# A perceiver layer on one core: first products regrouped, a slice of the shared expert by seven products, ranks computed earlier, two weight loads in chunks

## The chip, the cores and the metric

The kernel runs on one core of a Trainium2 chip. The time is the device time of that core in microseconds, as the median over several runs. One run was profiled: its time and the span of its trace are given beside each other below.

## The reference

The layer updates 256 tokens `x` of width 512 in three steps, all in float32. A layernorm without weights goes ahead of each step.

```python
x = x + xattn(layernorm(x), ctx, ctx)   # ctx: 25088 rows of width 512
x = x + attn(layernorm(x))              # 16 heads of 64, one key/value head, causal
x = x + ffn(layernorm(x))               # shared expert + top 8 of 64 experts

# xattn: qp = q@Wq.T+bq (128 wide), kp = k@Wk.T+bk, vp = v@Wv.T+bv
#        sigmoid(qp@kp.T / sqrt(128)) @ vp
# ffn:   shared = (silu(h@Sg) * (h@Su)) @ Sd * sigmoid(h@shared_gate)      inner width 1024
#        w, idx = top_k(softmax(h@gate_w), 8), w divided by its sum
#        expert e: (silu(h@Ge) * (h@Ue)) @ De, inner width 256, weighted by w
```

## The kernel before

**Cross attention** takes up most of the time. The context is cut into groups: group 0 has 128 rows (`HEAD`), groups 1 to 65 have 384 rows, three blocks of 128. For each group the keys are `pk = Wk @ context.T` (`keys`, eight matmul records of width 384 for a full group), evicted by ScalarE with the bias to `kT` (L362). The scores of a block are one product of a 128-column piece of `kT` with the queries `qT`; ScalarE applies the sigmoid and writes `zT` (L380). The value product `zT.T @ context` has 256 x 384 x 512 terms in blocks of 2 x 3 x 3 and is done with 15 block products instead of 18 (`PRODUCTS`, six PSUM banks named `xacc`): VectorE, GpSimd and ScalarE form sums of context blocks (`T`) and VectorE sums of score blocks (`S`). Group 0 has one block and only seven products (`FIRST_PRODUCTS`). The order of everything here is written out by hand: `in_turn` pins an instruction behind what was traced before it on its engine. In iteration `g` TensorE does the scores of the group's first two blocks, four products of the group before, the scores of the third block, the keys of group `g + 1`, then the other products of the group before. In iteration 1 the group before is group 0. VectorE turns group `g + 2`'s rows around in 32 x 32 squares (`quarters` to `cT`, L317) at the end of an iteration; the first two groups are turned by TensorE.

The loads of context go out on SP's queue, three groups ahead (`load_quarters`, four transfers, and `load_context`, one). The weights of later stages are fetched on the same queue during the cross attention: `later` makes a tile and a `fetch` that first lets GpSimd copy one element of the current `zT` into the tile's first element and then issues the transfers, so that they do not start early. `wvT` (1 MB) is fetched in group 6 and `a_wqT` (2 MB) in group 8. All of SP's transfers share that queue.

**Self attention** follows (from about 560 to 607 us), then routing and the **feed-forward stage**. Here most instructions are not pinned: the compiler's scheduler orders each engine's stream by when it expects operands. A shared expert of inner width 1024 is treated as four slices ("s", 0) to ("s", 3) of width 256, then eight experts ("e", 0) to ("e", 7) chosen by count are computed for all tokens ("whole" experts), with seven further experts (`FEW`) for a few gathered tokens. For each, `gate_up` makes 32 records of width 256 in two PSUM banks, ScalarE a sigmoid, VectorE two multiplications (L1217, L1218). `down` then multiplies with the down weights. For names in `SEVEN` the hidden values are first scaled per token (L1220), and the 2 x 2 block product is done in seven products of width 256 instead of eight: `sums_for_seven` forms four sums of weights on GpSimd (`t_s`, `t_e`) and four sums of hidden blocks on VectorE (`s_s`, `s_e`), the products accumulate in two double banks (`seven`), and `add_seven` adds them to `y` once, at the end. The scale of the shared slices is one row, written to memory by `turn_weights` and read back by a transfer on GpSimd's queue. Slice 0 is not in `SEVEN`: it goes down in four products of width 512 (`pd_s`, L1372), weighted by VectorE into `y` (L1381), and its gate products are made early (`ph_first`). `run` makes the next name's hidden values before the last one's down projection.

[...] In this stage four of them are handed out in turn by `bank`, so which instruction waits for which depends on the order of the calls.

`counted` ranks the 64 experts by their tokens, `permuted` gathers the weights in that order (`wso`). `seated`, called after expert 0's `gate_up`, counts each token's rank within each of the few experts (products `pn`, `rank`), compares it with the slot numbers (`share`, in the tile `fTf`), transposes that (`pt_share`) and gathers the tokens' rows by an indirect transfer. The weights of slices and experts rotate through three rooms (`wpool`), so slice 3's loads wait for slice 0's rooms, expert 0's for slice 1's, and so on.

Of the kernel before, what the change touches and what calls it, by code (L numbers as in the profile page):

```python
# [9 lines left out]
F32 = mybir.dt.float32  # L10
AF = mybir.ActivationFunctionType
ALU = mybir.AluOpType
# [9 lines left out]
def tile_perceiver_layer(  # L22
# [82 lines left out]
    def rows(src):  # L105
        return src.rearrange("(c p) f -> p c f", p=P)
# [7 lines left out]
    def blocks_of(g):  # L114

        return range(J) if g > 0 else (1,)
# [57 lines left out]
    def all_of(src):  # L174
        return (lambda t: t), src

    wvT_sb, fetch_wv = later("wvT", [P, ND, D], all_of(rows(wvT)))
    bv_sb, fetch_bv = later("bv", [P, D], all_of(bv[0].partition_broadcast(P)))
    a_wqT_sb, fetch_aq = later("a_wqT", [P, ND, INNER], all_of(rows(a_wqT)))
    a_wkv_sb, fetch_akv = later("a_wkv", [P, ND, 2 * DH], all_of(rows(a_wkvT)))  # L180
    a_wout_sb, fetch_aout = later("a_wout", [P, NE, D], all_of(rows(a_woutT)))
    ln_g_sb, fetch_lng = later("ln_g", [P, ND], all_of(ln_g))
# [162 lines left out]
    def keys(g):  # L345

        cT = turned_tiles.pop(g)
        n = len(blocks_of(g)) * P
        w = wkT_sb if g >= BY_PE else wk_plain_sb
        pk = keys_bank(f"pk_{g}")[:, 0:n]  # L350
        for c in range(ND):
            in_turn(
                nc.tensor.matmul(  # L353
                    pk,
                    lhsT=w[:, c, :],
                    rhs=cT[:, c, 0 : n // R, :].rearrange("p b r -> p (b r)"),
                    start=(c == 0),
                    stop=(c == ND - 1),
                )
            )  # L360
        kT = cpool.tile([QK, J * P], F32, tag="kT", name=f"kT_{g}")
        in_turn(nc.scalar.activation(kT[:, 0:n], pk, AF.Identity, bias=bk_sb))  # L362
        return kT

    def scores(g, kT, zT, blocks):
# [262 lines left out]
    for g in range(G):  # L628
        if g + 3 < G:
            load_quarters(g + 3)  # L630
            load_context(g + 3)
        named.z = zT = cpool.tile([P, J, T], F32, tag="zT", name=f"zT_{g}", bufs=3)
        context_sums(g, named)
        blocks = blocks_of(g)
        scores(g, kT, zT, blocks[0:2])
        if before is not None:
            values(before, 0, 4)
        if len(blocks) > 2:
            scores(g, kT, zT, blocks[2:3])
        if g + 1 < G:  # L640
            kT = keys(g + 1)
        if before is not None:
            values(before, 4)
        query_sums(g, named)
        if BY_PE <= g + 2 < G:
            turn(g + 2)
        for fetch in in_group.get(g, ()):
            fetch(zT[0:1, 0, 0:1])
        before, named = named, Named(g + 1)
        if g + 1 < G:  # L650
            context_sums_aside(g + 1, named)
# [140 lines left out]

    SEVEN = [("s", k) for k in range(1, NS)] + [("e", k) for k in range(WHOLE - 1)]
    LAST = ("e", WHOLE - 1)
    weights = {}
    scales = {}
# [377 lines left out]
    def turn_weights():  # L1177
        pt = bank("pt_wt")
        for t in range(NT):
            nc.tensor.transpose(pt[0 : E + 1, t * P : (t + 1) * P], wt[:, t, :], ident)  # L1180
        nc.vector.tensor_copy(wT, pt[0 : E + 1, :T])
        nc.gpsimd.dma_start(weights_of_tokens, wT)
        nc.gpsimd.dma_start(*spread(scale_rooms[0], slice(E, E + 1)))
        for k in range(1, NS):
            scales["s", k] = scale_rooms[0]

    def gate_up_products(n, halves, lo, hi, mark=lambda ins: ins):
        gu, _ = weights[n]
        for half, ph in enumerate(halves):
            if half > 0 and n == SEVEN[0]:  # L1190
                turn_weights()
            for f in range(NI):
                col = half * I + f * P
                for c in range(ND):
                    mark(
                        nc.tensor.matmul(  # L1196
                            ph[:, f * T + lo : f * T + hi],
                            lhsT=gu[:, c, col : col + P],
                            rhs=fT[:, c, lo:hi],
                            start=(c == 0),  # L1200
                            stop=(c == ND - 1),
                        )
                    )

    def gate_up(n, tiles_done=None):

        nm = f"{n[0]}{n[1]}"
        if tiles_done is None:
            halves = [bank(f"ph_{nm}_{half}") for half in range(2)]
            gate_up_products(n, halves, 0, T)  # L1210
        else:
            halves = tiles_done
        pg, pu = halves
        hT = hidden.tile([P, NI, T], F32, tag="hT", name=f"hT_{nm}")
        hf = hT.rearrange("p f t -> p (f t)")
        nc.scalar.activation(hf, pg, AF.Sigmoid)
        nc.vector.tensor_mul(hf, pg, hf)  # L1217
        nc.vector.tensor_mul(hf, pu, hf)  # L1218
        if n in SEVEN:
            nc.vector.tensor_mul(hT, hT, scales.pop(n).unsqueeze(1).to_broadcast([P, NI, T]))  # L1220
            sums_of[n] = sums_for_seven(n, hT)
        elif n == LAST:
            nc.vector.tensor_mul(hT, hT, scales.pop(n).unsqueeze(1).to_broadcast([P, NI, T]))
        return hT

# [33 lines left out]
        y11 y11 + u3  # L1261
    """
    HALF = D // 2
    sums_of = {}
    spread_out = {}
    seven = []

    def block(n, hT, dn, s, t, nm):
        i, k = nm[1:2], nm[2:3]
# [80 lines left out]
    def down(n, hT, parts=WIDE_PARTS):  # L1350
        if n in SEVEN:
            down_by_seven(n, hT)
            return
        _, dn = weights.pop(n)
        if n == LAST:
            for t, lo, hi in parts:
                pd = spread_out.pop((t, lo))
                for f in range(NI):
                    nc.tensor.matmul(  # L1359
                        pd,  # L1360
                        lhsT=hT[:, f, t * P : (t + 1) * P],
                        rhs=dn[:, f, lo:hi],
                        start=False,
                        stop=(f == NI - 1),
                    )
                nc.vector.tensor_add(y[:, t, lo:hi], pd, y[:, t, lo:hi])
            return
        nm = f"{n[0]}{n[1]}"
        for t, lo, hi in parts:
            pd = bank(f"pd_{nm}_{t}_{lo}")[:, 0 : hi - lo]  # L1370
            for f in range(NI):
                nc.tensor.matmul(  # L1372
                    pd,
                    lhsT=hT[:, f, t * P : (t + 1) * P],
                    rhs=dn[:, f, lo:hi],
                    start=(f == 0),
                    stop=(f == NI - 1),
                )
            w = wsh[:, t, :] if n[0] == "s" else wso[:, t, n[1] : n[1] + 1]
            so_far = x2 if n == ("s", 0) else y  # L1380
            nc.vector.scalar_tensor_tensor(  # L1381
                y[:, t, lo:hi], pd, w, so_far[:, t, lo:hi], ALU.mult, ALU.add
            )

    def run(names, between, last=WIDE_PARTS):

        pending = None
        for i, n in enumerate(names):
            hT = gate_up(n, first if n == ("s", 0) else None)
            if pending is not None:  # L1390
                down(*pending)
            pending = (n, hT)
            if i in between:
                between[i]()
        down(*pending, last)


    order = late.tile([1, E], mybir.dt.int32, tag="order", name="order")
# [105 lines left out]
            yield k, first, n * QUARTER  # L1504
            first += n * QUARTER

    def seated():


        w = wso[:, :, WHOLE : WHOLE + FEW]  # L1510
        chose = few.tile([P, NT, FEW], F32, tag="chose", name="chose")
        nc.vector.tensor_scalar(chose, w, 0.0, None, ALU.is_gt)
        ahead = few.tile([P, P], F32, tag="ahead", name="ahead")
# [4 lines left out]
        for t in range(NT):  # L1518
            for s in range(t + 1):
# [4 lines left out]
                    start=(s == 0),  # L1524
                    stop=(s == t),
                )

        rank = few.tile([P, NT, FEW], F32, tag="rank", name="rank")
        nc.vector.scalar_tensor_tensor(  # L1529
            rank.rearrange("p t i -> p (t i)"),  # L1530
            pn[:, 0 : NT * FEW],
# [3 lines left out]
            ALU.mult,  # L1535
        )
        nc.vector.tensor_scalar(rank, rank, 1.0, None, ALU.subtract)
        for t in range(NT):
            for r in range(NR):
                for k, first, n in slots_of_round(r):  # L1540
                    i = k - WHOLE
                    nc.vector.tensor_scalar(
                        share[:, t, r, first : first + n],
                        slot_sb[:, 0:n],
                        rank[:, t, i : i + 1],
                        w[:, t, i : i + 1],
                        ALU.is_equal,
                        ALU.mult,
                    )
# [128 lines left out]

    def few_added(r):
        for t, i, room in parts_of_round(r):  # L1680
            in_turn(
                nc.vector.scalar_tensor_tensor(
                    y[:, t, :], room, fetched_w[:, t, i : i + 1], y[:, t, :], ALU.mult, ALU.add
                )
            )

# [36 lines left out]
    def remaining(lo):  # L1723
# [5 lines left out]
        with tc.If(n_left > lo):  # L1729
            places(lo, hi, by=ACT)  # L1730
            store(nc.scalar, WIDE_PARTS)
            remaining(hi)

    places(
        0,
        WHOLE,
# [90 lines left out]
```

## Time and profile before

| | us |
|---|---|
| median of 3 runs (769.94 to 770.69) | 770.08 |
| the profiled execution: its time | 770.29 |
| its span in the trace | 768.5 |
| TensorE busy | 758.1 |
| VectorE busy | 565.3 |
| ScalarE busy | 201.2 |
| GpSimd busy | 198.2 |

The mean granted TensorE clock is 0.997 of full speed. In the profile, PE is TensorE's matmuls and PEld its weight loads, DVE is VectorE, ACT ScalarE, POOL GpSimd, and SPq the queue of transfers that SP issues. A float32 product shows as two records. Line numbers such as L353 are those of the kernel before. The span divides into the cross attention (to about 550 us), the change to the value projection and self attention (to about 607), the output normalisation and routing (to about 625), the shared slices (625 to 660), the experts (660 to 757) and the last sums and stores.

### The profile page before, as it was taken

Reading aid. Unit: us, or ns where it says so; the run is one execution under the profiler, and the core shown is the slowest. Engines: PE = TensorE matmul, PEld = TensorE weight load, DVE = VectorE, ACT = ScalarE, POOL = GpSimd, SP = SyncE. Lnnn points to the kernel's source line nnn. Section 1 sums busy time; section 2 is a strip of 40 time slices with the busy share of each in tenths; the row PEclk is TensorE's granted clock in tenths of the full one; section 3 lists DMA queues with packets and bytes.
Section 4 is the critical chain, followed back from the end, with each engine's and each line's share of the span. In section 5 each row is a group of like instructions: output and inputs, shape, how many; then the busy total and the mean of one; then the engine's idle time right before and its main releaser. Section 6 shows DMA issues by size and latency. Waiting matters only on the chain.

```text
span 768.5 us, 12420 instructions
## 1 busy us (share of the span) xinstructions
PE 758.1 (99%) x4056; PEld 619.8 (81%) x4056; DVE 565.3 (74%) x1652; ACT 201.2 (26%) x485; POOL 198.2 (26%) x361
## 2 busy tenths in 40 slices
PE   8999999999999999999999999999999999999996
PEld 6888888888888888888888888888876588887665
DVE  5988888888888888888888888888666575442353
ACT  4222222222222222222222222222346430010110
POOL 3222322322322322322322322322124213151150
PEclk9999999999999999999999999999999999999998
DMA  9999999899778778878778778770060025569940
GB/s 249 269 236 252 255 205 295 241 228 222 187 181 209 186 185 208 185 182 209 185 185 208 184 185 204 187 185 22 21 226 1 15 77 174 178 217 397 385 145 31
DMA packets 155190, 145.92 MB, mean 190 GB/s; under 512 B 7926, under 2 KB 113667, under 8 KB 155120
## 3 DMA queue, kind: packets, MB, share of 16 engines
q1 hardware_dynamic: 153088, 140.41, 70.4%
q0 software_dynamic: 1360, 4.13, 1.8%
q8 instruction: 34, 0.56, 0.3%
q10 hardware_dynamic: 672, 0.52, 0.2%
q14 instruction: 36, 0.29, 0.1%
HBM read 143.40 MB, written 1.64 MB: 189 GB/s over the span
## 4 chain that ended last, share of the span: by engine, by line
PE 97%; DVE 1%; ACT 0%; POOL 0%; issue 0%; ACTq 0%
PE xacc L572 37%; PE pk L353 22%; PE pz L371 11%; PE ph_e L1196 7%; PE seven L1302 4%; PE ph_s L1196 3%; PE pw L937 2%; PE pa L871 2%; PE ph_few L1618 1%; PE ps L963 1%; PE ptp L1014 1%; PE pi L204 1%; PE po_few L1649 1%; PE py L731 1%; PE ph_first L1196 0%; PE pd_few L1359 0%
## 5 line engine op out<-in xcount | busy, mean ns | idle before, releaser
L572 PE MATMUL xacc<-T,S 128*128 128x172 f32 (+2 forms) x912 | 185.5, 308 | 0.0
L353 PE MATMUL pk<-cT,wkT_sb 128*128 128x384 f32 x512 | 175.5, 486 | 0.0
L572 PEld LDWEIGHTS xacc<-T,S 128*128 128x128 f32 x912 | 152.6, 190 | 20.3
L353 PEld LDWEIGHTS pk<-cT,wkT_sb 128*128 128x128 f32 x512 | 97.1, 190 | 54.4
L539 POOL TENSOR_TENSOR T<-ctx 128x172 f32<-128x172 f32 x65 | 31.9, 491 | 384.9 <-PE xacc L572 379.3
L317 DVE STREAM_TRANSPOSE cT<-quarters 128x1536 f32<-128x1536 f32 x64 | 113.4, 1772 | 0.3 <-issue 0.2
L539 DVE TENSOR_TENSOR T<-ctx 128x172 f32<-128x172 f32 (+1 forms) x262 | 113.3, 433 | 0.0
L539 DVE TENSOR_TENSOR S<-zT 128x128 f32<-128x128 f32 x196 | 56.4, 288 | 72.2 <-ACT zT L380 72.2
L371 PE MATMUL pz<-qT,kT 128*128 128x256 f32 x392 | 106.0, 379 | 0.7 <-ACT kT L362 0.7
L380 ACT ACTIVATE zT<-pz 128x256 f32<-128x256 f32 (+1 forms) x131 | 64.2, 490 | 114.1 <-PE pz L371 114.1
L572 PE MATMUL xacc<-T,zT 128*128 128x173 f32 (+1 forms) x396 | 89.9, 308 | 0.0
L572 PE MATMUL xacc<-ctx,S 128*128 128x172 f32 x392 | 78.5, 309 | 0.0
L362 ACT ACTIVATE kT<-pk,bk 128x384 f32<-128x384 f32 (+1 forms) x66 | 38.1, 578 | 146.9 <-PE pk L353 146.9
L539 DVE TENSOR_TENSOR S<-zT,S 128x128 f32<-128x128 f32 x325 | 76.4, 285 | 0.0
L549 ACT COPY T<-ctx 128x170 f32<-128x170 f32 (+1 forms) x130 | 43.2, 333 | 125.4 <-PE xacc L572 124.0
L539 POOL TENSOR_TENSOR T<-ctx,T 128x170 f32<-128x170 f32 (+1 forms) x130 | 72.5, 576 | 2.2 <-PE xacc L572 2.2
L371 PEld LDWEIGHTS pz<-qT,kT 128*128 128x128 f32 x392 | 68.6, 190 | 4.8 <-ACT kT L362 1.3
L539 DVE TENSOR_TENSOR T<-ctx,T 128x172 f32<-128x172 f32 x195 | 65.4, 361 | 8.2 <-PE xacc L572 1.5
L572 PEld LDWEIGHTS xacc<-T,zT 128*128 128x128 f32 x396 | 66.4, 190 | 0.1
L572 PEld LDWEIGHTS xacc<-ctx,S 128*128 128x128 f32 x392 | 62.8, 190 | 0.0
L572 PE MATMUL xacc<-ctx,zT 128*128 128x170 f32 (+1 forms) x264 | 59.5, 307 | 0.0
L1196 PE MATMUL ph_e<-fT,gu 128*128 128x256 f32 x256 | 58.0, 382 | 0.3 <-DVE rank L1529 0.3
(297 smaller groups left out, 778.0 us busy)
## 6 DMA issues: line engine op xcount, KB each, us to landing
ctx<-in_context SPq DMA_DIRECT2D x65, 768.0 KB, 5.4
quarters<-in_context SPq DMA_DIRECT2D x256, 192.0 KB, 6.4
gu<-in_e_gate_up SPq DMA_DIRECT2D x12, 1024.0 KB, 9.9
dn<-in_e_down SPq DMA_DIRECT2D x11, 512.0 KB, 9.4
gu_s<-in_s_gate_up SPq DMA_DIRECT2D x8, 512.0 KB, 4.6
a_wqT<-in_a_wqT SPq DMA_DIRECT2D x1, 2048.0 KB, 15.6
a_wout<-in_a_woutT SPq DMA_DIRECT2D x1, 2048.0 KB, 15.6
dn_s<-in_s_down SPq DMA_DIRECT2D x4, 512.0 KB, 7.5
```

The source lines that it names most:

```text
L317: in_turn(nc.vector.transpose(new_turned(g), q.rearrange("p b (c r) -> p c b r", r=R)))
L353: nc.tensor.matmul(pk, lhsT=w[:, c, :], rhs=cT[:, c, 0 : n // R, :].rearrange("p b r -> p (b r)"), start=(c == 0), stop=(c == ND - 1),)
L362: in_turn(nc.scalar.activation(kT[:, 0:n], pk, AF.Identity, bias=bk_sb))
L371: nc.tensor.matmul(pz[:, i * T : (i + 1) * T], lhsT=kT[:, at : at + P], rhs=qT, start=True, stop=True,)
L380: nc.scalar.activation(zT[:, blocks[0] : blocks[-1] + 1, :].rearrange("p j t -> p (j t)"), pz[:, 0 : len(blocks) * T], AF.Sigmoid, scale=1 ...
L539: in_turn(f(o_, a_, b_))
L549: in_turn(nc.scalar.copy(named[to][:, 0:n], named[x_][:, 0:n]))
L572: nc.tensor.matmul(banks_of_products[i][:, cols], lhsT=named[lhs], rhs=named[rhs][:, 0:n],  start=i not in opened, stop=(g == G - 1 and last),
L871: nc.tensor.matmul(pa[:, 0 : hi - lo], lhsT=a_wqT_sb[:, c, e * P : (e + 1) * P], rhs=anT[:, c, lo:hi], start=(c == 0), stop=(c == ND - 1),)
L937: nc.tensor.matmul(pw[t], lhsT=oT[:, e, t * P : (t + 1) * P], rhs=a_wout_sb[:, e, :], start=(e == 0), stop=(e == NE - 1),)
L1196: nc.tensor.matmul(ph[:, f * T + lo : f * T + hi], lhsT=gu[:, c, col : col + P], rhs=fT[:, c, lo:hi], start=(c == 0), stop=(c == ND - 1),)
L1302: nc.tensor.matmul(product_of_seven(nm), lhsT=block(n, hT, dn, s_, t_, lhs), rhs=block(n, hT, dn, s_, t_, rhs),  start=(n == SEVEN[0] and ...
```

## The change

Four places change.

1. Iteration 1 of the cross attention deals the seven products of group 0 differently: two ahead of group 1's first scores, three between its scores, two after the next keys. The evictions of the keys of groups 1 and 2 are done in two pieces, the first 128 columns and then the others.
2. `wvT` and `a_wqT` are loaded by four transfers each, one for each chunk of 128 input rows, instead of one each.
3. Slice ("s", 0) joins `SEVEN`. Its scaling and its sums are made in slice 1's `gate_up`, ahead of slice 1's own (`weigh`), and its down projection follows slice 2's `gate_up`, with slice 1's behind it. `y` is no longer written by slice 0; the first of the few experts' additions takes `x2` in its place.
4. The part of `seated` that computes `rank` becomes `ranked_tokens`, called ahead of the whole experts' stage.

```diff
+    def by_chunks(src):
+        return [
+            ((lambda t, c=c: t[:, c, :]), src[c * P : (c + 1) * P, :]) for c in range(ND)
+        ]
-    wvT_sb, fetch_wv = later("wvT", [P, ND, D], all_of(rows(wvT)))
+    wvT_sb, fetch_wv = later("wvT", [P, ND, D], *by_chunks(wvT))
-    a_wqT_sb, fetch_aq = later("a_wqT", [P, ND, INNER], all_of(rows(a_wqT)))
+    a_wqT_sb, fetch_aq = later("a_wqT", [P, ND, INNER], *by_chunks(a_wqT))
...
-        in_turn(nc.scalar.activation(kT[:, 0:n], pk, AF.Identity, bias=bk_sb))
+        for lo, hi in ((0, P), (P, n)) if 0 < g < 3 else ((0, n),):
+            in_turn(nc.scalar.activation(kT[:, lo:hi], pk[:, lo:hi], AF.Identity, bias=bk_sb))
...
+        early, middle = (2, 5) if g == 1 else (0, 4)
+        if before is not None:
+            values(before, 0, early)
         scores(g, kT, zT, blocks[0:2])
         if before is not None:
-            values(before, 0, 4)
+            values(before, early, middle)
...
-            values(before, 4)
+            values(before, middle)
...
-    SEVEN = [("s", k) for k in range(1, NS)] + [("e", k) for k in range(WHOLE - 1)]
+    SEVEN = [("s", k) for k in range(NS)] + [("e", k) for k in range(WHOLE - 1)]
...
-            if half > 0 and n == SEVEN[0]:
+            if half > 0 and n == ("s", 1):
                 turn_weights()
...
+        if n == ("s", 1):
+            weigh(*waiting)
+        if n in SEVEN + [LAST] and n != ("s", 0):
+            weigh(n, hT)
+        return hT
+
+    def weigh(n, hT):
+        nc.vector.tensor_mul(hT, hT, scales.pop(n).unsqueeze(1).to_broadcast([P, NI, T]))
         if n in SEVEN:
-            nc.vector.tensor_mul(hT, hT, scales.pop(n).unsqueeze(1).to_broadcast([P, NI, T]))
             sums_of[n] = sums_for_seven(n, hT)
...
-        pending = None
+        pending = []
         for i, n in enumerate(names):
             hT = gate_up(n, first if n == ("s", 0) else None)
-            if pending is not None:
-                down(*pending)
-            pending = (n, hT)
+            if n == ("s", 0):
+                waiting.extend((n, hT))
+            elif n != ("s", 1):
+                for each in pending:
+                    down(*each)
+                pending = []
+            pending.append((n, hT))
...
-    def seated():
+    rank = few.tile([P, NT, FEW], F32, tag="rank", name="rank")
+    w = wso[:, :, WHOLE : WHOLE + FEW]
+
+    def ranked_tokens():
...
+            so_far = x2 if (r, i) == (0, ROUNDS[0][0][0] - WHOLE) else y
...
+    ranked_tokens()
     places(
```

More of the change, by code (lines that the diff above doesn't have):

```diff
@@ L1183, in turn_weights @@
         nc.gpsimd.dma_start(*spread(scale_rooms[0], slice(E, E + 1)))
-        for k in range(1, NS):
+        for k in range(NS):
             scales["s", k] = scale_rooms[0]
@@ L1218, in gate_up @@
         nc.vector.tensor_mul(hf, pu, hf)
+        if n == ("s", 1):
[5 more added lines that the diff above has]
+        nc.vector.tensor_mul(hT, hT, scales.pop(n).unsqueeze(1).to_broadcast([P, NI, T]))
         if n in SEVEN:
-            nc.vector.tensor_mul(hT, hT, scales.pop(n).unsqueeze(1).to_broadcast([P, NI, T]))
             sums_of[n] = sums_for_seven(n, hT)
-        elif n == LAST:
-            nc.vector.tensor_mul(hT, hT, scales.pop(n).unsqueeze(1).to_broadcast([P, NI, T]))
-        return hT
     S_OF_SEVEN = """
@@ L1263, in tile_perceiver_layer @@
     HALF = D // 2
+    spread_out = {}
     sums_of = {}
-    spread_out = {}
-    seven = []
+    seven, waiting = [], []
     def block(n, hT, dn, s, t, nm):
@@ L1378, in down @@
                 )
-            w = wsh[:, t, :] if n[0] == "s" else wso[:, t, n[1] : n[1] + 1]
-            so_far = x2 if n == ("s", 0) else y
+            w = wso[:, t, n[1] : n[1] + 1]
             nc.vector.scalar_tensor_tensor(
-                y[:, t, lo:hi], pd, w, so_far[:, t, lo:hi], ALU.mult, ALU.add
+                y[:, t, lo:hi], pd, w, y[:, t, lo:hi], ALU.mult, ALU.add
             )
     def run(names, between, last=WIDE_PARTS):
-        pending = None
+        pending = []
         for i, n in enumerate(names):
             hT = gate_up(n, first if n == ("s", 0) else None)
-            if pending is not None:
-                down(*pending)
-            pending = (n, hT)
+            if n == ("s", 0):
[5 more added lines that the diff above has]
+            pending.append((n, hT))
             if i in between:
                 between[i]()
-        down(*pending, last)
+        for each in pending:
+            down(*each, last)
     order = late.tile([1, E], mybir.dt.int32, tag="order", name="order")
@@ L1505, in slots_of_round @@
             first += n * QUARTER
-    def seated():
-        w = wso[:, :, WHOLE : WHOLE + FEW]
+    rank = few.tile([P, NT, FEW], F32, tag="rank", name="rank")
+    w = wso[:, :, WHOLE : WHOLE + FEW]
+    def ranked_tokens():
         chose = few.tile([P, NT, FEW], F32, tag="chose", name="chose")
@@ L1526, in seated @@
                 )
-        rank = few.tile([P, NT, FEW], F32, tag="rank", name="rank")
         nc.vector.scalar_tensor_tensor(
@@ L1537, in seated @@
         nc.vector.tensor_scalar(rank, rank, 1.0, None, ALU.subtract)
+    def seated():
         for t in range(NT):
@@ L1680, in few_added @@
         for t, i, room in parts_of_round(r):
+            so_far = x2 if (r, i) == (0, ROUNDS[0][0][0] - WHOLE) else y
             in_turn(
                 nc.vector.scalar_tensor_tensor(
-                    y[:, t, :], room, fetched_w[:, t, i : i + 1], y[:, t, :], ALU.mult, ALU.add
+                    y[:, t, :], room, fetched_w[:, t, i : i + 1], so_far[:, t, :], ALU.mult, ALU.add
                 )
```

## The prediction

> **What bounds the kernel now.** I read the page first, then the chain of waits, then TensorE's timeline at the places that the diff touches.
>
> ```profile
> PE 758.1 (99%) x4056; PEld 619.8 (81%) x4056; DVE 565.3 (74%) x1652; ACT 201.2 (26%) x485; POOL 198.2 (26%) x361
> ...
> PE 97%; DVE 1%; ACT 0%; POOL 0%; issue 0%; ACTq 0%
> ```
>
> The first line is the busy time of each engine, the second the chain that ended last, by engine. TensorE carries 97% of the chain, so only two things can move the end: TensorE work that goes, and one of its few holes. Next, TensorE's waits between 8 and 700 us (total, times, longest):
>
> ```profile
> PE pz L371 <- ACT kT L362: 0.7, 1, 0.7
> ...
> PE ph_e L1196 <- DVE rank L1529: 0.3, 1, 0.3
> ```
>
> Both holes lie where the diff works. TensorE's timeline at the first (start, duration, instruction), and the chain in order of time at the second (start, duration, what):
>
> ```profile
> 12.54 2.74 PE L353 MATMUL pk<-cT,wk_plain 128*128 128x384 f32 x8
> 15.95 1.13 PE L371 MATMUL pz<-qT,kT 128*128 128x256 f32 x4 [0.67 <-ACT kT L362]
> 16.92 0.45 PE L572 MATMUL xacc<-T,zT 128*128 128x170 f32 x2
> ```
>
> ```profile
> 632.23 3.43 PE pd_s L1372 x8
> 635.67 6.91 PE ph_s L1196 x32
> 642.57 3.02 PE seven L1302 x14
> ...
> 659.78 6.92 PE ph_e L1196 x32
> 666.70 0.02 issue
> 666.72 0.60 DVE hT_e L1218
> 667.33 0.01 issue
> 667.33 0.17 DVE rank L1529
> 667.50 0.04 issue
> 667.55 2.42 PE ph_e L1196 x10
> ```
>
> At 15 us the scores of group 1 wait for the eviction of their keys. At 632 us the first shared slice goes down in four wide products (two records each, as every product here). At 666 us expert 1 waits until VectorE has multiplied expert 0's second half and computed `rank`.
>
> [...] the 256-wide `ph_s` has a mean of 382 ns, yet 32 of them take 6.91 us, 0.216 us apart. I price TensorE by spacing. [...] two `s_s` sums took 0.70 us each beside the GpSimd sums at 637.6, and the sums after 644 took 0.29. [...]
>
> **Part 1: first group's products, keys in pieces.** No product is added; all three places are in TensorE's written order. Before: `pk` ends at 12.54 + 8 x 0.3225 = 15.12, the scores start at 15.95 and the first pays 0.10 more than the spacing. That is 0.93 lost. After: two products of group 0 come first. Four records at (18.08 - 16.92)/8 = 0.145 make 0.58, to 15.70. They need `zT` (ready 13.12) and the sums `T` (13.35). The eviction started at 15.32; its first piece has the form of the 128-wide one that took 0.35 at 10.31, so it is done at 15.67 and seen at 15.72. The second, 256 wide, lies between 0.35 and 0.58, overlaps the first a little and ends near 16.05; the second block's scores want it at 16.15 or later. Left: 0.02 and the slow start, 0.10. One group on, the cover shrinks from three products (0.87) to two (0.58). Before: eviction starts 0.27 after `pk` ends, takes 0.58, is seen after 0.05, so 0.90 against 0.87. After: 0.27 + 0.35 + 0.05 = 0.67 against 0.58, 0.09 lost instead of 0.03. **Sum: 0.93 + 0.03 - 0.12 - 0.09 = 0.75 us gained**, bounds 0.3 (the first scores wait for both pieces) and 0.85. Pieces do release early in this kernel: at 552.11 `py` starts on the first of three copies of `zcT` that run to 552.50. ScalarE pays one more instruction in two groups and is idle there for over 2 us.
>
> Does the lead survive? VectorE's S sums of group 1 end 0.6 earlier, near 20.8, but the quarters of group 3, issued to 14.05 with up to 7.0 to landing, arrive near 21.0. The transpose, late by 0.3, is done at 22.8; TensorE wants it at 24.55 - 0.75 = 23.8. Later groups run at TensorE's pace with VectorE idle about 1 us in each (72.2 us before S in the page, over 64 groups).
>
> **Part 2: two loads in four chunks each.** Same bytes, same queue, six more issues on SP at 0.39 to 1.3 us each (rows of `wvT`, `a_wqT`). Behind them on SP wait the quarters of the next group. At `a_wqT` those landed near 93.2, 15.2 after issue, and the transpose started at 93.38, just then; it ends at 95.2 and `pk` of that group starts at 98.8. So 3.6 us of slack, 2.8 with TensorE ahead, cover the issues. **0**, bounds -0.1 and +0.3, unless the chunks run ahead (rival 1).
>
> **Part 3: first slice in seven products.** TensorE loses `pd_s`, 3.43, and gains 14 records as in the row `seven`, 3.02: **0.41 gained**. VectorE loses two `y` operations (0.73 + 0.74) and gains one multiplication (0.67) and four S sums (1.44 + 0.28 + 0.27 beside GpSimd). GpSimd gains four T sums of 0.73. What hides these: TensorE now goes from slice 1 (ends 632.2) straight to slice 2, until 639.1. Slice 0's scale row lands at 631.95 + 3.6 = 635.6, as before; VectorE is then working off the count until 636.2, multiplies until 636.9 and has S by about 639.3. The first S is wanted six records into `seven`, at 640.4: 1.1 us of slack. T of slice 0 runs 632.5 to 635.4. Slice 1's S and T follow by 641.2 and 638.9, wanted at 643.4. Moved with it: `dn_s` of slice 3, on SP, whose room comes free with the first down projection; issue goes from 635.70 to about 642.2. It landed 4.7 after issue, so 647; its T sums end near 650 and `seven` of slice 3 comes at 656. The expert load at 632.83 already stands ahead of it on SP; the next waits for slice 1's room, about 645, as before. If it came to stand behind, its 6.2 to landing gives 648.5, wanted at 659. Cost 0, up to 1.0 if VectorE is late. Taking `x2` in `few_added` instead changes an operand only.
>
> **Part 4: ranks ahead.** `chose` has been ready since 648.2, so the six tiny `pn` records can stand before expert 0, (666.89 - 666.66)/2 = 0.11 apart: 0.65. The two rank operations leave the hole at 666.7, as does the dependence of expert 1's bank on `rank`. Counting the helper's PSUM banks in the new order, expert 1's first half takes the bank of expert 0's second half, so it still waits for L1218: 0.93 from the last product to the restart. But the slot comparisons (14 at about 0.21) can now run in VectorE's 7.65 us idle time before 663.9, so the six `pt_share` transposes (0.11 each, 0.65) fit into that hole instead of being dealt into expert 1. Before: from expert 0's end, 666.52, to `seven` at 675.63, 9.10. After: 0.93 + 0.10 + 6.91 + 0.65 for `pn` elsewhere = 8.60. **0.50 gained.** If the transposes don't fall into the hole, 0.65 more: 0.15 lost. If a different bank frees expert 1, up to 0.8 gained. The gather on GpSimd moves up as well; its T sums behind it come sooner.
>
> **Sum.** 0.75 + 0.41 + 0.50 = 1.66. Against the profiled execution: span 768.5, its time 770.29, so 1.8 lies outside the span and stays; 768.6 after. That run stands 0.2 above the median 770.08; against the median **768.4 us**.
>
> **Rivals.** (1) *The chunks run ahead; slower.* The marker that holds a load back writes only element 0, that is chunk 0. Chunks 1 to 3 (three quarters of 1024 and 2048 KB, 2.36 MB) do not touch it and could be issued in the first microseconds. At the 260 to 280 GB/s of those stretches they take 8.7 us, all ahead of context. The quarters of group 3, transposed by 22.8 and wanted at 23.8, have 1.0 us to spare, so it decides from about 0.27 MB ahead of them. With all of it TensorE stalls for 7.7 us: **776**. For it: the geometry. Against it: a load of before has the same form, `gates`, whose second part misses the marker, and it stayed in place:
>
> ```profile
> 151.61 0.39 SPq L170 DMA_DIRECT2D gates<-in_gate_w  x1
> 152.22 0.38 SPq L170 DMA_DIRECT2D gates<-in_sgate_w  x1
> ```
>
> (2) *The hole at 666 stays empty*: part 4 gives -0.15, total 1.0, **769.1**. For it: TensorE's order past the cross stage is not all written out, and the transposes may be put inside expert 0. (3) *A new wait takes the gain*: slice 0's S late by 1 us, or the scores waiting for both pieces; two thirds of the gain or less remain, **769.3** to 770.
>
> **How the numbers follow.** Forecast with all three gains 0.55; rival 2, 0.20; rival 3, 0.15; rival 1, 0.10. A measurement can tell about 0.2%, 1.54 us: the line is 768.54, close to the forecast. Of the first case I count 0.85 beyond it, a little of rival 2: faster 0.49. Slower is rival 1 alone with a little for stalls that I don't see: 0.11. Within 0.2%: 0.40. Range 767.4 (upper bounds of parts 1 and 4 and some more) to 770.3 (rival 3 whole); rival 1 is left out.
>
> **What would show it.** Right: `pz` at about 15.7 without a wait of 0.7 for `kT`; `pk` of group 3 near 23.8 instead of 24.55; the cross stage's last product 0.75 earlier; no `pd_s`, 56 records of `seven` from four slices; `dn_s` issued near 642 less the lead; `pt_share` between the experts 0 and 1. Wrong: `wvT` or `a_wqT` on SP before 50 us, VectorE's transpose waiting for quarters with TensorE idle behind it, a wait of `seven` for `s_s`, or `ph_e` idle for 0.9 at expert 1.

## The result, and the profile after

The changed kernel takes 768.33 us (median of 11 runs, 767.92 to 768.92), the kernel before 770.32 beside it (11 runs, 769.94 to 770.79). The ratio is 0.9973, with a 95% interval of 0.9964 to 0.9981: 1.99 us, about 0.26%, faster. The profiled execution took 768.20, its span is 766.3.

The busy line of the page after, which answers to the one shown of before:

```profile
PE 756.8 (99%) x4062; PEld 620.7 (81%) x4062; DVE 569.1 (74%) x1655; ACT 201.3 (26%) x487; POOL 203.8 (27%) x365
```

TensorE is still the bound. It issues six records more and is busy 1.3 us less. TensorE's timeline at the first hole (start, duration, instruction), and the records of the kernel before that answer to its first, fifth and last line:

```profile
11.87 0.60 PE L378 MATMUL pz<-qT,kT 128*128 128x256 f32 x2
...
14.88 0.45 PE L579 MATMUL xacc<-T,zT 128*128 128x170 f32 x2
15.17 0.46 PE L579 MATMUL xacc<-ctx,zT 128*128 128x172 f32 x2
15.50 1.13 PE L378 MATMUL pz<-qT,kT 128*128 128x256 f32 x4
...
17.34 0.68 PE L378 MATMUL pz<-qT,kT 128*128 128x256 f32 x2
...
23.68 2.74 PE L358 MATMUL pk<-cT,wkT_sb 128*128 128x384 f32 x8
```

```profile
12.11 0.60 PE L371 MATMUL pz<-qT,kT 128*128 128x256 f32 x2
...
18.08 0.59 PE L371 MATMUL pz<-qT,kT 128*128 128x256 f32 x2
...
24.55 2.74 PE L353 MATMUL pk<-cT,wkT_sb 128*128 128x384 f32 x8
```

Two products of group 0 stand between the keys and the scores, and the wait of 0.67 for `kT` has left the list of waits. From the first scores to the keys of group 3 the stretch is 11.81 (23.68 - 11.87), where it was 12.44 (24.55 - 12.11). One line is for later: the third block's two score records, at 17.34, take 0.68 where they took 0.59 (at 18.08). The chain in order of time at the shared slices, then at the experts 0 and 1:

```profile
627.91 10.36 PE ph_s L1207 x48
638.27 6.04 PE seven L1318 x28
```

```profile
658.50 0.57 PE pn L1541 x6
659.06 7.01 PE ph_e L1207 x32
666.07 0.23 PE pt_share L1576 x2
...
666.38 0.38 ACT shareT L1577
666.77 0.04 issue
666.81 7.17 PE ph_e L1207 x32
673.98 3.02 PE seven L1318 x14
```

There is no `pd_s`; the slices 0 and 1 go down one behind the other in 28 records of `seven`. `pn` stands ahead of expert 0, and `pt_share` in the hole behind it. The hole is still there: from 665.91, where expert 0's last product leaves TensorE, to 666.81 it is 0.90. The same stretch took 1.03 before (666.52 to 667.55), with the six records of `pn` in it. By the profile, what ends it is now ScalarE's copy of `pt_share`.

**Where the 2.18 us between the two spans come from.** The table cuts every traced run at the same five places of TensorE's timeline (us): start of the first scores `pz`; from there to the first record of group 3's keys; to `pp`; to `seven` of expert 0; TensorE's last end to the end of the span. The stretch left out, from `seven` of expert 0 to TensorE's last end, is 86.68 in all of them. "Looks" is the time from the last landing of `out` until SP has looked at its last transfer semaphore and goes on to its next instruction.

| run | first scores | to keys of 3 | to `pp` | to `seven` of e0 | tail | looks | median time |
|---|---|---|---|---|---|---|---|
| before | 12.11 | 12.44 | 620.98 | 30.10 | 6.21 | 0.53 | 770.32 |
| changed | 11.87 | 11.81 | 620.57 | 29.58 | 5.84 | 0.08 | 768.33 |
| c3 changed again | 12.22 | 11.81 | 620.55 | 29.58 | 5.65 | 0.08 | 768.22 |
| a1 part 1 alone | 12.20 | 11.81 | 620.96 | 30.10 | 6.17 | 0.54 | 769.76 |
| a2 part 2 alone | 12.08 | 12.44 | 620.96 | 30.09 | 5.58 | 0.08 | 769.82 |
| a3 part 3 alone | 12.19 | 12.44 | 620.54 | 30.10 | 6.22 | 0.54 | 770.03 |
| a4 part 4 alone | 12.50 | 12.44 | 620.99 | 29.58 | 6.42 | 0.53 | 770.21 |
| b1 whole keys | 12.05 | 12.24 | 620.96 | 30.10 | 5.50 | 0.53 | 770.17 |
| b2 three transfers more | 12.38 | 12.44 | 620.96 | 30.09 | 5.62 | 0.29 | 770.08 |
| b3 changed, one more | 12.08 | 11.81 | 620.55 | 29.58 | 6.38 | 0.63 | 768.65 |
| b4 slice 3 carried | 12.36 | 11.81 | 620.53 | 29.23 | 5.64 | 0.08 | 768.16 |
| c1 chunks early | 12.09 | 16.21 | 623.30 | 29.58 | 5.71 | 0.08 | 774.48 |
| c2 carried, two sigmoids | 11.78 | 11.87 | 620.53 | 29.23 | 5.77 | 0.08 | 767.73 |

Before to changed: 0.24 at the start, 0.63 in part 1's stretch, 0.41 in part 3's, 0.52 in part 4's, 0.37 in the tail; with rounding 2.18. The middle three repeat to 0.04 in every kernel that has the part as it is, c1 apart. The start scatters from run to run (11.78 to 12.50, in no order with the edits) and is no gain. The tail scatters as well, from 5.50 to 6.42; how much of its 0.37 belongs to the change is taken up with the kernels b2 and b3. The ratios below are each to the kernel before run beside it, whose medians were 770.31 to 770.43.

### The profile page after: what moved, and what is told of

It is laid out like the page before. It is cut to its first block, busy times and chain, and to the rows that moved or that the text cites. A ratio compares the mean times of both kernels' runs of the same rounds, so it can differ in the third digit from the quotient of the medians.

```text
span 766.3 us, 12454 instructions
## 1 busy us (share of the span) xinstructions
PE 756.8 (99%) x4062; PEld 620.7 (81%) x4062; DVE 569.1 (74%) x1655; ACT 201.3 (26%) x487; POOL 203.8 (27%) x365
## 4 chain that ended last, share of the span: by engine, by line
PE 95%; DVE 2%; ACT 1%; POOL 1%; DMA 0%; issue 0%; ACTq 0%; DVEq 0%; POOLq 0%
PE xacc L579 37%; PE pk L358 22%; PE pz L378 11%; PE ph_e L1207 7%; PE seven L1318 4%; PE ph_s L1207 3%; PE pa L882 2%; PE pw L948 1%; PE ph_few L1641 1%; PE ps L974 1%; PE po_few L1672 1%; PE py L743 1%; PE ptp L1025 1%; POOL pe L1011 1%; PE ph_first L1207 0%; DMA x_sb<-in_x 0%
## 5 line engine op out<-in xcount | busy, mean ns | idle before, releaser
L369 ACT ACTIVATE kT<-pk,bk 128x384 f32<-128x384 f32 (+2 forms) x68 | 38.4, 568 | 146.9 <-PE pk L358 146.9
```

Source lines behind the costliest of these rows:

```text
L369: in_turn(nc.scalar.activation(kT[:, lo:hi], pk[:, lo:hi], AF.Identity, bias=bk_sb))
```

## The experiments

**Each part alone.** Four kernels, each the kernel before with one part of the diff shown above.

> The kernel before with part 1 alone (group 0's products dealt 2, 3, 2 and the keys of groups 1 and 2 evicted in two pieces). Theory (each part gains by itself, and the 0.24 us by which the changed kernel's first scores started earlier, 11.87 against 12.11, is not part 1's): from the first scores to the keys of group 3 the stretch takes 11.81 instead of 12.44 us, 0.63 less, and stays so to the end: about 769.7. Rival A (the earlier start belongs to the change): first scores at 11.87 again and the keys of group 3 at 23.7. Rival B (the prediction's own 0.75): the stretch takes 11.69.

769.76, ratio 0.9993 (0.9985 to 1.0001). The stretch takes 11.81, as in the changed kernel, and the first scores start at 12.20. So part 1 is worth 0.63, both rivals fall, and the early start does not belong to part 1.

> The kernel before with part 2 alone (wvT and a_wqT loaded by four transfers each). Theory: time unchanged within 0.3 us, since TensorE never waits for what stands behind them; the chunks of a_wqT are issued near 73 to 75 and the last lands near 84, where the one transfer of before landed at 89.1, and the quarters behind it land near 88 instead of 93.2. Rival A (the earlier landing in the changed kernel came from its other parts): landing near 89 and 93 as before. Rival B (the chunks run ahead of the context once nothing else moves them): first context groups late, 776.

769.82, ratio 0.9992 (0.9983 to 1.0000). Nothing ran ahead: the chunks of `a_wqT` were issued from about 73 us on. The last landed at 86.32 and the quarters behind them at 89.94, between the two theories, and no stretch of TensorE changed. But the tail is 0.63 shorter: 0.45 of that are SP's looks, as in the changed kernel, and for the other 0.18 the last store landed sooner after its issue (3.38 in place of 3.56). The theory of no effect falls; b2 and b3 below take that up.

> The kernel before with part 3 alone (the first shared slice in seven products). Theory: TensorE has 14 records of 0.216 us in place of 8 of 0.43, so 0.41 less from the first slice to the product pp, and that to the end: about 769.9; GpSimd's four more sums cost TensorE nothing. Rival (VectorE's scaling and sums of two slices stand one behind the other and seven waits for them): a wait of seven for s_s of up to 1 us, time 770.3 to 770.9.

770.03, ratio 0.9994 (0.9986 to 1.0002). `pp` comes 0.44 earlier, and no wait for `s_s` is among TensorE's waits. The chain there has the form of the changed kernel:

```profile
628.84 10.36 PE ph_s L1195 x48
639.21 6.04 PE seven L1306 x28
```

> The kernel before with part 4 alone (ranks computed ahead of the whole experts). Theory: six pt_share records lie in the hole between expert 0's last product and expert 1's first, which lasts 0.90; pn takes 0.57 between slice 3 and expert 0; seven of expert 0 starts 0.53 earlier relative to slice 3's last product: about 769.8. In this hole the first record of expert 1 is one of its second half, in a bank of pt_share, and it starts after ScalarE's copy shareT. Rival (the banks are handed out in another order without part 3, and the transposes fall inside expert 1): 0.15 slower.

770.21, ratio 0.9996 (0.9988 to 1.0004); its time alone would not tell 0.5 from nothing, its timeline does. `seven` of expert 0 comes 0.52 earlier, and the hole is the same without part 3:

```profile
667.60 0.82 PE L1556 MATMUL pt_share<-ident,fTf 128*128 128x128 f32 x6
668.50 7.17 PE L1196 MATMUL ph_e<-fT,gu 128*128 128x256 f32 x32
```

Why ScalarE ends it I read from the order of the built program, and no view of the profile shows it: expert 1's first record there belongs to its second half, in a PSUM bank that `pt_share` has just left, and waits for ScalarE; the record after it belongs to the first half and waits for VectorE. Both come free within 0.05 (copy done at 666.76, VectorE's multiplication of expert 0's second half at 666.81 in the changed kernel), so the hole would be about as long with either.

**The pieces of the keys, left out.** Part 1's deal of products without its eviction in pieces; the diff is against a1.

```diff
-        for lo, hi in ((0, P), (P, n)) if 0 < g < 3 else ((0, n),):
-            in_turn(nc.scalar.activation(kT[:, lo:hi], pk[:, lo:hi], AF.Identity, bias=bk_sb))
+        in_turn(nc.scalar.activation(kT[:, 0:n], pk, AF.Identity, bias=bk_sb))
```

> The kernel before with group 0's products dealt 2, 3, 2 but the keys of groups 1 and 2 evicted whole. Theory (the pieces carry most of part 1: a whole eviction takes 0.27 to start, 0.58 and 0.05 to be seen, 0.90 against a cover of two products, 0.58): TensorE idle for about 0.3 ahead of the first scores of group 1 and again of group 2; the stretch from the first scores to the keys of group 3 about 12.3 us, against 12.44 before and 11.81 with pieces, a gain of 0.1 to 0.2. Rival (the products alone are the gain, the pieces hardly matter): 11.9 or less.

770.17, ratio 0.9999 (0.9991 to 1.0007); the stretch takes 12.24. TensorE's timeline ahead of the scores of group 2, with the wait that the pieces remove:

```profile
20.83 0.45 PE L572 MATMUL xacc<-ctx,zT 128*128 128x170 f32 x2
21.12 0.45 PE L572 MATMUL xacc<-T,zT 128*128 128x171 f32 x2
21.73 1.13 PE L371 MATMUL pz<-qT,kT 128*128 128x256 f32 x4 [0.15 <-ACT kT L362]
```

From 21.12 the two records take 0.29, so 0.32 are lost here, and 0.26 at group 1. The deal alone gains 0.20, the pieces on top of it 0.43. The pieces without the deal were not run.

**The tail.** At the end SP waits for its eight transfer semaphores, places 0 to 7. In the traces the last landing, that of the last store of `out`, is counted by place 1 before, and by place 7 with the six transfers more of part 2. As I read it, transfers take the places in turn and SP looks at them in that order, so the number of transfers in the whole program decides how many looks come after the last store. The counts below fit that. Here are SP's semaphore instructions of that line after the last landing (766.36 and 764.62), of before and of the changed kernel (count, durations in ns, first and last start):

```profile
L1729 SPq EVENT_SEMAPHORE  x7: 17/17/17, 766.4 to 766.8; - x7
```

```profile
L1754 SPq EVENT_SEMAPHORE  x1: 17/17/17, 764.6 to 764.6; - x1
```

Before, seven of the eight come after the landing, one of them the last store's own; now only that one. Two kernels move the place with a load that part 2 does not touch, by splitting `a_wkv` in four (b2, from before) or in two (b3, from the changed kernel). The edit of b2; that of b3 takes two chunks at a time:

```diff
-    a_wkv_sb, fetch_akv = later("a_wkv", [P, ND, 2 * DH], all_of(rows(a_wkvT)))
+    a_wkv_sb, fetch_akv = later("a_wkv", [P, ND, 2 * DH], *(
+        ((lambda t, c=c: t[:, c : c + 1, :]), rows(a_wkvT)[:, c : c + 1, :])
+        for c in range(0, ND, 1)))
```

> The kernel before with a_wkv, another load, in four transfers in place of one, nothing else: three more transfers, so the last store of the output is counted by the semaphore at place 4 of 0 to 7 in place of place 1. Theory (at the end SP looks at its eight transfer semaphores in their order, 0.07 to 0.075 us each, and what stands behind the last store's own comes after its landing): three places left in place of six, from the last landing to the end 1.94 us, between 2.16 before and 1.72 with the chunks of part 2; time about 770.2. Rival (the shorter end belongs to the two chunked loads themselves, or is scatter of the runs): 2.16.

> The changed kernel with a_wkv in two transfers in place of one, nothing else: one more transfer, and the last store moves on to place 0, so seven places are left to look at. Theory: from the last landing to the end 2.2 us in place of 1.72, the kernel 0.5 slower than the changed one: about 768.8. Rival (no matter of places): 1.72 and 768.3.

The same row of the profile of b2 (landing at 765.90) and of b3 (764.81):

```profile
L1736 SPq EVENT_SEMAPHORE  x4: 17/17/17, 765.9 to 766.1; - x4
```

```profile
L1761 SPq EVENT_SEMAPHORE  x8: 17/17/17, 764.8 to 765.4; - x8
```

Looks of 0.08, 0.29, 0.53 and 0.63 for one, four, seven and eight of them: the ladder is as expected, with another load split in b2 and b3 than in part 2. From the last landing to the end b3 takes 2.26, as expected, and b2 2.27 in place of 1.94: there VectorE, which reached its closing semaphore 3.1 us after its last branch in place of 2.9, came later than SP, and SP waited 0.37 for it. The kernel b4 below has one look and still takes 2.28, with a wait of 0.59. SP's waits for VectorE in b2 and in b4 (total, times, longest):

```profile
SPq L1830 <- DVEq L1736: 0.4, 1, 0.4
```

```profile
SPq L1855 <- DVEq L1759: 0.6, 1, 0.6
```

In these two the last store landed 2.9 us after its issue, and in b1 after 2.8, against 3.4 to 3.8 in all the others. With seven looks b1 has the shortest tail of all, 5.50. So in b2 and b4 VectorE's end was a floor close below, and as I read it the 0.45 of part 2 comes off the whole time only where the last store lands late. The times, 770.08 (1.0000, 0.9993 to 1.0008) and 768.65 (0.9980, 0.9973 to 0.9988; 0.32 slower than the 768.33 of the changed kernel), go the right way without proving it.

**Slice 3 carried.** Since the hole at expert 1 stays, this kernel puts work into it: slice 3's down projection goes behind expert 0's hidden values. `run` is made to return what has not gone down yet (`keep`) and to start with it later (`pending`); two of its places, shortened:

```diff
-    run([("s", k) for k in range(NS)], {0: counted, 1: load_first, 2: permuted})
+    carried = run([("s", k) for k in range(NS)], {0: counted, 1: load_first, 2: permuted}, keep=True)
...
+        pending=carried,
```

> The changed kernel with slice 3's down projection (14 records of seven, 3.02 us) put behind expert 0's hidden values, where the hole between the experts 0 and 1 is, in place of ahead of expert 0. Theory: the hole of 0.90 us closes, the six pt_share (0.65) that lay in it now cost their own time, so 0.25 earlier than the changed kernel from there on: about 768.1. Rival A: the weights of expert 2, which wait for slice 3's room, come later, and TensorE waits for them, 0.5 or more slower than the changed kernel. Rival B: TensorE waits for the slot comparisons or the copy of pt_share in any case, no difference.

768.16 (8 runs), ratio 0.9973 (0.9963 to 0.9983). `seven` of expert 0 comes 0.35 earlier than in the changed kernel, and the hole is gone:

```profile
665.93 0.59 PE L1318 MATMUL seven<-dn_s,s_s 128*128 128x256 f32 x2
666.37 0.82 PE L1580 MATMUL pt_share<-ident,fTf 128*128 128x128 f32 x6
667.02 7.07 PE L1207 MATMUL ph_e<-fT,gu 128*128 128x256 f32 x32
```

0.25 of it as expected; the other 0.10 is the first record behind the hole, which was slow in the changed kernel (7.17 for the 32 records, here 7.07). No wait of TensorE for expert 2's weights followed, so both rivals fall. The median, 0.17 below the changed kernel's, would not tell it.

**Rival 1 carried out.** The chunks 1 to 3 of both loads are issued at once, ahead of the quarters of group 3.

```diff
+        if name in ("wvT", "a_wqT"):
+            for to, src in parts[1:]:
+                nc.sync.dma_start(to(t), src)
+            parts = parts[0:1]
```

> The changed kernel with chunks 1 to 3 of wvT and a_wqT (2.36 MB) really issued ahead of the quarters of group 3, the case of the prediction's rival 1. Theory: they stand in the same transfers' way for 8.7 us at the rate of that stretch, the quarters of group 3 land some 8 us later, TensorE stalls for 7.7 ahead of the keys of group 3: 776 against 768.3. Rival (the groups behind have enough ahead to make it up, or the rate is higher): 770 or less.

774.48 (5 runs), ratio 1.0061 (1.0047 to 1.0075); the profiled execution took 775.39. TensorE's one wait between 8 and 110 us, and stretches of its timeline (window; busy us and instructions of PE, PEld, DVE, ACT, POOL; granted clock; DMA share; GB/s):

```profile
PE pk L362 <- DVE cT L326: 4.2, 1, 4.2
```

```profile
20.00:23.50 3.50, 3.50 (x20) 2.91 (x19) 1.39 (x7) 1.78 (x5) 0.00 (x0) 1.00 1.12 308
28.20:33.50 5.30, 5.21 (x8) 2.86 (x9) 4.53 (x20) 0.00 (x0) 0.00 (x0) 0.50 1.16 272
```

VectorE's transpose of group 3 waited 5.07 for the quarters and started at 26.46, where it started at 21.14 in the changed kernel. In the kernel before, the DMA share was already 1.14 to 1.17 between 12 and 42 us, at 261 to 279 GB/s. The stall costs 4.4, not 7.7: the bytes moved at 402 to 419 GB/s from 15 to 21 us, not at 260 to 280. Behind it the eight records of `pk` are 0.64 apart (the first 0.80) in place of 0.32, at a granted clock of 0.50: another 2.7. The group after that is at its usual pace, and nothing is made up. So it was right that the chunks delay the quarters and that this costs time, and in the profiled execution two errors in the price nearly cancelled, 7.1 against 7.7. The median is 0.91 below that execution. The three fastest of the five ran at a mean granted clock of 0.995 to 0.996, the profiled one at 0.994, which by my estimate from these means fits a shorter stretch at half clock; against the changed kernel (c3, 768.22) the price is 6.3.

**The sigmoid in two pieces.** In the changed kernel the third block's scores of group 1 begin to load their weights at 17.32, just behind the end of the sigmoid of the first two blocks (16.67 + 0.60 = 17.26); their first record takes 0.30 to the next instead of 0.22. All scores share one bank. This kernel is b4 with that sigmoid cut in two; the edit, shortened:

```diff
+        pieces = [blocks[0:1], blocks[1:]] if g == 1 and len(blocks) > 1 else [blocks]
+        for some in pieces:
...
```

> The kernel with slice 3's down projection carried past expert 0, and group 1's sigmoid of its first two blocks in two pieces. Theory: the third block's scores of group 1 wait for that sigmoid (one bank for all scores; 16.67 + 0.60, seen at 17.32 in the changed kernel), which cost 0.08 that the prediction left out; with a first piece done by about 16.5 the three products between the scores cover it, so the stretch from the first scores to the keys of group 3 takes 11.73 in place of 11.81 us, and the kernel about 768.0. Rival (the 0.08 is not that wait): 11.81.

767.73 (7 runs), ratio 0.9969 (0.9958 to 0.9980). The 0.08 is not gained back: the stretch takes 11.87.

```profile
17.30 0.70 PE L378 MATMUL pz<-qT,kT 128*128 128x256 f32 x2
```

Counted from the first scores, the second piece ends at 5.46 (17.245 - 11.784) where the whole sigmoid ended at 5.40 (17.264 - 11.865), and in both kernels the weights of the third block's scores start 0.05 behind that end. So the wait is for the sigmoid, as supposed, but for all of it: that its first piece would do is refuted, and the second instruction's cost, 0.06, came on top. From the first scores to TensorE's last end this kernel (748.31) is no shorter than b4 (748.25), so these two traces give no reason for its lower median; start and tail scatter by as much.

> The changed kernel as it is, beside the others on the same chip. Theory: about 768.3, first scores anywhere between 11.9 and 12.5 us (the start scatters from run to run), 11.81 from there to the keys of group 3, and 0.08 from the last landing to the end of SP's looking at its semaphores, as in its first profile. Rival (the early start, 11.87, belongs to the change): 11.87 again.

768.22 (12 runs), ratio 0.9973 (0.9965 to 0.9982), first scores at 12.22. All as the theory had it: the parts repeat, the early start does not.

## Why the prediction was right, and where it was not

**The total** came within 0.07 of the 768.4 that was forecast, and that is luck in part. The sum was 0.33 too small, 1.66 for the 1.99 measured, and it was taken from 770.08, the median of three runs; over eleven runs the kernel before stands at 770.32, 0.24 higher. In the sum, part 1 was 0.12 too large, and what was missing is part 2, which was put at 0. The table's terms give 0.63 + 0.41 + 0.52 + 0.45 = 2.01, the last of them the most that SP's looks give. The medians of the four parts alone lie 0.67, 0.61, 0.40 and 0.22 below the kernel before beside them, 1.90 together, each uncertain by about 0.6.

**Part 1**, 0.75 predicted, 0.63 found. The term that failed is "left: 0.02 and the slow start, 0.10" at group 1. The first scores lose 0.04, not 0.02, and the third block's scores lose 0.08 that the sum did not have: with three products between the scores in place of four, the cover of the first blocks' sigmoid is used up. Group 2's first scores start 0.39 behind the start of the last product ahead of them (20.72 to 21.11), where they started 0.32 behind it (21.67 to 21.99): 0.07 lost, where 0.06 was counted. That the pieces release early was right; on top of the deal they are two thirds of the part, as b1 shows. `pk` of group 3 stood at 23.68 (predicted "near 23.8"), 0.24 of its lead being the start.

**Part 2**, 0 predicted with bounds of -0.1 and +0.3; it is worth up to 0.45 at the end of the program. The step looked for an effect where the transfers are issued and at what stands behind them, and there it was right: the issues are hidden, and the chunks came behind the marker, as `gates` had. Whether the marker itself holds chunks 1 to 3, or only their place on SP behind chunk 0, no run separates. The step did not ask what the *number* of transfers changes. a2, b2 and b3 show it: the place of the last store in SP's closing row of waits. Rival 1 did not come, and c1 shows that its price was real: 6.3 us, where 7.6 was forecast (776 against 768.4).

**Part 3**, 0.41 predicted, 0.41 to 0.44 found, with no wait for the sums. The cover was at least as wide as said: all eight S sums of the slices 0 and 1 were done at 638.25, `seven` started at 638.27. One detail went the other way round. The first two sums on VectorE were expected to be slow beside GpSimd, 1.44. They took 0.47, and a GpSimd sum took 3.52 instead. Slice 1's T sums were done at 640.2 in place of 638.9, still ahead of their use. `dn_s` was issued at 641.38 and landed in 3.5; GpSimd waited 1.0 for it, TensorE did not.

**Part 4**, 0.50 predicted, 0.52 found. The transposes fell into the hole (rival 2 fell). `pn` cost 0.66, against 0.65: its six records take 0.57, and the 32 records of `ph_e` behind them 7.01 where they took 6.92. The hole measured 0.90 against 0.93. The releaser named for it was not the one: by the profile the first record behind the hole waited for ScalarE's copy, and VectorE's multiplication was done only 0.05 after that copy. By the reading given with a4, the count of the banks missed that the scheduler puts one record of expert 1's second half first.

**Rival 3**, a new wait that takes two thirds of the gain, did not come; the one new wait of TensorE that the sum did not have is the 0.08.

## What to carry to other kernels

Price a product by its spacing to the next (0.216 us for `ph_s`, where its mean duration is 382 ns). Where one engine is the bound and its order is known, a gain of half a microsecond in 770 could here be told in advance to about 0.1 us. Compare stretches between marks on the bounding engine, not totals, since start (0.72) and tail (0.92) alone scatter by more than any part here is worth. Before moving work to cover an eviction, go through every wait that the moved work covered before. Where a change alters how many transfers a program issues, look at the closing waits as well as at the queue.

## What the runs showed of the hardware that I had not expected

**SP's closing looks cost time one by one**: 0.07 to 0.10 us for each transfer semaphore still to be looked at after the last landing, 0.08 to 0.63 in all by the place of the last store. In b2 and b4, where that store landed 2.9 us after its issue, SP then still waited 0.37 and 0.59 for VectorE.

**The stall of TensorE in c1 cost twice.** TensorE stood idle for 4.2 us, in a stretch with a mean granted clock of 0.85 (23.5 to 28.2 us), and then ran 5.3 us at 0.50; from 33.5 to 40 us the clock was 0.99. By the spacing of the records the stall cost 4.4 and the slow stretch another 2.7. The hole of 0.90 at expert 1 cost only the 0.10 of the first record behind it.

**A GpSimd sum took 3.52 us beside a run of VectorE instructions.** GpSimd's timeline of the changed kernel, then VectorE's at both ends of the run:

```profile
634.52 0.73 POOL L1302 TENSOR_TENSOR t_s<-dn_s 128x256 f32<-128x256 f32 x1
635.33 3.52 POOL L1302 TENSOR_TENSOR t_s<-dn_s,t_s 128x256 f32<-128x256 f32 x1
```

```profile
635.36 1.27 DVE L1238 TENSOR_TENSOR hT_s<-hT_s,wqT 128x512 f32<-128x512 f32 x2
...
638.18 0.67 DVE L1228 TENSOR_TENSOR hT_s<-ph_s,hT_s 128x512 f32<-128x512 f32 x1
```

From 635.36 to 638.25 VectorE ran two multiplications and eight sums without a gap. a3 and c3 have the same 3.52. GpSimd's sum started at 635.33 and ended at 638.85, 0.67 after VectorE had gone on to L1228 at 638.18; the sum ahead of it and the one behind it took 0.73 each. So it looks as if the run held GpSimd off from first to last and the sum was done behind it. That is my estimate from these times, and no run tests it.
